# Weighted sums of layer 0: transposes by VectorE in squares of 32 instead of by TensorE, and steps in other units

## The chip, the cores and the metric

The kernel runs on one core of a Trainium2 chip, in float32 throughout. The metric is the time of one execution on the device in microseconds (us); the median of several runs counts. The core's engines work side by side, each through its own queue in program order, and wait for one another through semaphores: TensorE (PE in the profile; its weight loads are PEld), VectorE (DVE), ScalarE (ACT), GpSimd (POOL) and SyncE (SP), which here only issues DMAs. TensorE's results land in PSUM[...]; the other data are in SBUF.

## The reference

The model has two layers, each an attention and a feed-forward part with a layernorm ahead and a residual sum behind. The change lies in the first attention:

```
def _L0_attn_ref(x, Wqkv, bqkv, Wout, bout):      # 16 heads of 8
    B, S, D = x.shape                             # 16, 256, 128
    qkv = (x @ Wqkv + bqkv).reshape(B, S, 3, NUM_HEADS, HEAD_DIM)
    qkv = jnp.transpose(qkv, (2, 0, 3, 1, 4))
    q, k, v = (qkv[0] * SCALE, qkv[1], qkv[2])
    scores = jnp.einsum('bhqd,bhkd->bhqk', q, k)
    attn = jax.nn.softmax(scores, axis=-1)
    out = jnp.einsum('bhqk,bhkd->bhqd', attn, v)
    out = jnp.transpose(out, (0, 2, 1, 3)).reshape(B, S, D)
    return out @ Wout + bout
...
    x = L0_attn_x
    x = x + _L0_attn_ref(_layernorm(x, axis=-1), L0_attn_Wqkv, ...)
    x = x + _L0_ffn_ref(_layernorm(x, axis=-1), ...)
```

The feed-forward part of layer 0 is a gated recurrence over the batch index: from one batch of 256 rows to the next, `c = sigmoid(f) * c + sigmoid(i) * tanh(g)`, where f, i and g are products of the normalised rows and of the old `c` with weights. Each batch thus needs three gates, and the `c` of the batch before. The second layer (linear attention with rotary positions, then a mixture of experts) is not touched.

## The kernel before

The first stage takes the attention of layer 0 and the recurrence together, as a pipeline over 16 batches. An outer loop over `n` runs from -3 to 17, and an inner one over eight units (the table `UNITS`, lines 470 to 479). In each unit `scores` (L333) is issued first, and then the steps that the table lists for that unit; an entry such as `(project, -1)` is `project` for batch n-1. The program is issued in just this order (`manual_schedule`), so the table fixes each engine's order.

`scores` does a quarter of a group of heads at a time, twice. For batch n+1 it computes queries by keys (`pm`, L352, eight matmul records on TensorE in 32-row strips) and VectorE takes each query's maximum from it (`nmax`, L363). For batch n it computes keys by queries with the maxima in an extra row (`psc`, L358), and ScalarE takes the exponential (`pr`, L369). `pm` and `psc` share the pool `ps_me`: three buffers of two PSUM banks each, two of which are taken in each unit.

The other two banks are the pool `ps_x`, two buffers with the tag `misc`, through which everything else goes in turn:

- `stats` (L288): loads x three batches ahead (SP), takes mean and variance (VectorE L213, L214), the root (GpSimd L215, L216), and `xb` = x plus output bias (GpSimd L295). `normal` (L299) normalises (L222, VectorE), `flip` (L302) transposes (L233, TensorE; L234, ScalarE).
- `queries_keys` (L306): two matmuls (L310, L311), two ScalarE copies `qc` and `kc`, nine DMAs from SP which lay them out for `scores`. `values` (L323): two matmuls (L327) and a copy.
- `place_maxima` (L371): two transposes into `pt` (L376), a ScalarE copy `nmT` (L381), two DMAs from SP.
- `weighted` (L387): for four heads at a time, 16 matmul records `av` (L393). Heads lie 32 partitions apart; of each 32 rows, eight are weighted sums, the ninth is the sum of the weights (a column of ones in `va`), and the others are zero. ScalarE copies `av` into `oT` (L400).
- `divide` (L402): for each half of the 256 rows four transposes by TensorE into `po` (L408), then VectorE takes the reciprocal of the ninth columns (L413) and multiplies (L414) into `at`. `flip_heads` (L419) transposes `at` back on TensorE, and ScalarE copies it into `aT`.
- `project` (L423): two matmuls with `wo1` (L427), plus `xb` (VectorE L430) into `xr`, and the statistics of the next layernorm with the same helper as `stats`. `normal2` and `flip2` are as `normal` and `flip`.
- `gate` (L443): two matmuls (L445, L446; two records each) and a tanh on ScalarE. `forget` (L452, VectorE L454) and `update` (L458, VectorE L461 and L464) carry `c` on.

Then follows one product with the final `c` and the second layer, whose order a planner sets by costs.

Of the kernel before, what the change touches and what calls it, by code (L numbers as in the profile page):

```python
# [9 lines left out]
F32 = mybir.dt.float32  # L10
AF = mybir.ActivationFunctionType
ALU = mybir.AluOpType
# [3 lines left out]
B, S, D = 16, 256, 128  # L16
HEADS, HD = 16, 8
NG, GH, ROW = 4, 4, 32
GAP = ROW // HD
P = 128  # L20
NC_ = S // P
E, H, NHC = 16, 256, 2
# [88 lines left out]
def kernel(ctx: ExitStack, tc: tile.TileContext, a: dict, out: bass.AP):  # L111
    nc = tc.nc
# [28 lines left out]
    bv = load("bv", [P, 1])  # L141
    wo1 = load("wo1", [P, D])
    bo1 = load("bo1", [P, D], a["bo1"].partition_broadcast(P))
# [39 lines left out]
    ident = const.tile([P, P], F32, tag="ident", name="ident")  # L183
# [23 lines left out]
    def ln_stats(small, src):  # L207
        st = small.tile([P, NC_, 6], F32, tag="ln_st", name="ln_st")
        mv = small.tile([P, NC_, 2], F32, tag="ln_mv", name="ln_mv")
        ve = small.tile([P, NC_], F32, tag="ln_ve", name="ln_ve")  # L210
        rs = small.tile([P, NC_], F32, tag="ln_rs", name="ln_rs")
        for c in range(NC_):
            nc.vector.bn_stats(st[:, c, :], src[:, c, :])  # L213
            nc.vector.bn_aggr(mv[:, c, :], st[:, c, :])  # L214
        nc.gpsimd.tensor_scalar_add(ve, mv[:, :, 1], EPS)  # L215
        nc.gpsimd.tensor_tensor(rs, ve, mhalf, ALU.pow)  # L216
        return mv, rs

    def ln_apply(work, src, mv, rs, tag):
        y = work.tile([P, NC_, D], F32, tag=tag, name=tag)  # L220
        for c in range(NC_):
            nc.vector.tensor_scalar(  # L222
                y[:, c, :], src[:, c, :], mv[:, c, 0:1], rs[:, c : c + 1], ALU.subtract, ALU.mult
            )
        return y

    def layernorm(small, work, src, tag):
        return ln_apply(work, src, *ln_stats(small, src), tag)

    def transposed(ps_pool, src, dst):  # L230
        ps = ps_pool.tile([P, 512], F32, tag="misc", name="ps_tr")
        for c in range(NC_):
            nc.tensor.transpose(ps[:, c * P : (c + 1) * P], src[:, c, :], ident)  # L233
        nc.scalar.copy(dst, ps[:, :S])  # L234
# [7 lines left out]
    with ExitStack() as st:  # L242
        heads = st.enter_context(tc.tile_pool(name="heads", bufs=1))
        small = st.enter_context(tc.tile_pool(name="small", bufs=3))
        work = st.enter_context(tc.tile_pool(name="work", bufs=2))
# [3 lines left out]
        ps_x = st.enter_context(tc.tile_pool(name="ps_x", bufs=2, space=PSUM))  # L249
# [36 lines left out]
        now = {}  # L286
# [10 lines left out]
            )  # L297

        def normal(b):  # L299
            now["y1", b] = ln_apply(work, *now.pop(("ln1", b)), "ln1")  # L300

        def flip(b):  # L302
            yT = now["yT", b] = work.tile([P, S], F32, tag="yT", name="yT")
# [83 lines left out]
        def weighted(b, g):  # L387

            prs = [now.pop(("pr", b, 2 * g + i)) for i in range(2)]
            av = ps_x.tile([P, S], F32, tag="misc", name="av")  # L390
            for c in range(NC_):
                for j in range(GH):
                    nc.tensor.matmul(  # L393
                        av[ROW * j : ROW * (j + 1), :], lhsT=vas[b % 3][:, c, GH * g + j, :],
                        rhs=prs[j // 2][:, j % 2, c, :],
                        start=(c == 0), stop=(c == NC_ - 1),
                    )
            if g == 0:
                now["oT", b] = work.tile([P, NG, S], F32, tag="oT", name="oT")
            nc.scalar.copy(now["oT", b][:, g], av)  # L400

        def divide(b):  # L402
            oT = now.pop(("oT", b))
            at = now["at", b] = work.tile([P, NC_, D], F32, tag="at", name="at")
            for c in range(NC_):
                po = ps_x.tile([P, HEADS, ROW], F32, tag="misc", name="po")
                for g in range(NG):
                    nc.tensor.transpose(  # L408
                        po[:, GH * g : GH * (g + 1), :].rearrange("p h r -> p (h r)"),
                        oT[:, g, c * P : (c + 1) * P], ident,  # L410
                    )
                rden = small.tile([P, HEADS], F32, tag="rden", name="rden")
                nc.vector.reciprocal(rden, po[:, :, HD])  # L413
                nc.vector.tensor_tensor(  # L414
                    at[:, c].rearrange("p (h d) -> p h d", d=HD), po[:, :, 0:HD],
                    rden.unsqueeze(2).to_broadcast([P, HEADS, HD]), ALU.mult,
                )

        def flip_heads(b):  # L419
            aT = now["aT", b] = work.tile([P, S], F32, tag="aT", name="aT")  # L420
            transposed(ps_x, now.pop(("at", b)), aT)

        def project(b):  # L423
            aT = now.pop(("aT", b))
# [6 lines left out]
            now["ln2", b] = xr[:, b], *ln_stats(small, xr[:, b])  # L431

        def normal2(b):
            now["y2", b] = ln_apply(work, *now.pop(("ln2", b)), "ln2")

        def flip2(b):
            transposed(ps_x, now.pop(("y2", b)), xT2[:, b])
# [20 lines left out]
        def update(b):  # L458
# [10 lines left out]

        UNITS = (  # L470
            ((weighted, -1, 3), (flip, 2), (forget, -2)),
            ((place_maxima, 0, 1), (divide, -1)),
            ((weighted, 0, 0), (flip_heads, -1), (stats, 3)),
            ((queries_keys, 2), (values, 2), (normal, 3)),
            ((weighted, 0, 1), (project, -1)),
            ((place_maxima, 1, 0), (gate, -2, 2), (normal2, -1)),
            ((weighted, 0, 2), (flip2, -1), (update, -2)),
            ((gate, -1, 0), (gate, -1, 1)),
        )
        with tc.manual_schedule():  # L480
            for n in range(-3, B + 2):
# [21 lines left out]
    with ExitStack() as st:  # L503
        small = st.enter_context(tc.tile_pool(name="small1", bufs=3))
# [29 lines left out]
        now = {}  # L534
# [599 lines left out]
    with ExitStack() as st:  # L1134
# [4 lines left out]
        now = {}  # L1139
# [72 lines left out]
def _laid_out(inp):  # L1212

    import numpy as np

    f = np.float32

    g = {k: np.asarray(v) for k, v in inp.items()}
    a = {"x": g["L0_attn_x"]}
    w, bias = g["L0_attn_Wqkv"], g["L0_attn_bqkv"]  # L1220
    a["wq"], a["wk"], a["wv"] = w[:, :D], w[:, D : 2 * D], w[:, 2 * D :]
    a["bq"], a["bk"], a["bv"] = (bias[i * D : (i + 1) * D, None] for i in range(3))
    a["wo1"], a["bo1"] = g["L0_attn_Wout"], g["L0_attn_bout"]

    gates = ("f", "i", "c")
    a["wg"] = np.stack([g[f"L0_ffn_w{i}"].T for i in gates], 1)
    a["ug"] = np.stack([g[f"L0_ffn_u{i}"].T for i in gates], 1)
    a["bg"] = np.stack([g[f"L0_ffn_b{i}"] for i in gates], 1)
    a["in_c"] = g["L0_ffn_in_c"][:, None]
    a["woT"], a["uoT"], a["bo"] = g["L0_ffn_wo"].T, g["L0_ffn_uo"].T, g["L0_ffn_bo"]  # L1230

    w = g["L1_attn_w_qkv"].T
    wq = w[:, :D].reshape(D, HEADS, 2, HD // 2)
    a["wq2"] = np.stack([wq.reshape(D, D), wq[:, :, ::-1].reshape(D, D)], 1)
    wk = w[:, D : 2 * D].reshape(D, HEADS, 2, HD // 2)
    a["wk2"] = np.concatenate([wk.reshape(D, D), wk[:, :, ::-1].reshape(D, D)], 1)
    a["wv2"] = w[:, 2 * D :]
    a["wo2"] = g["L1_attn_w_out"].T
    inv = (1.0 / f(10000.0) ** (np.arange(0, HD, 2, dtype=f) / f(HD))).astype(f)
    ang = np.arange(S, dtype=f)[:, None] * inv[None, :]  # L1240
    cos, sin = np.cos(ang).astype(f), np.sin(ang).astype(f)
    cos, sin = np.concatenate([cos, cos], 1), np.concatenate([-sin, sin], 1)
    turn = np.stack([cos, sin], 1)
    a["turnN"] = turn.reshape(NC_, P, 2, HD).transpose(1, 0, 2, 3)
    a["turnT"] = np.tile(turn.transpose(2, 1, 0) * f(HD**-0.5), (HEADS, 1, 1))
    head = np.arange(D) // HD
    a["bmask"] = np.concatenate(
        [head[:, None] == head[None, :], head[:, None] == np.arange(HEADS)[None, :]], 1
    ).astype(f)

    a["desc"] = np.arange(E, 0, -1).astype(f)
    a["wr"], a["br"] = g["L1_ffn_Wr"], g["L1_ffn_br"]
    a["b2"] = np.zeros((P, GT, D), f)
    for i in range(GT):
        a["b2"][i * E : (i + 1) * E, i] = g["L1_ffn_b2"]
    a["wx"] = np.concatenate(
        [
            g["L1_ffn_b1"].reshape(E, NHC, P).transpose(2, 0, 1),
            g["L1_ffn_W1"].transpose(1, 0, 2),
            g["L1_ffn_W2"].reshape(E, NHC, P, D).transpose(2, 0, 1, 3).reshape(P, E, NHC * D),  # L1260
        ],
        2,
    )
    n = np.arange(P, dtype=f)
    a["before"] = (n[:, None] < n[None, :]).astype(f)
    a["upto"] = (n[:E, None] <= n[None, :E]).astype(f)
    a["steps128"] = P * n[: 2 * E, None]
    a["numbers"], a["numbers128"] = n[:, None], P * n[:, None]
    a["first_row"], a["which"] = REGION * n[:E], n[:E]
    a["seen0"] = REGION // P * n[:E]  # L1270
    a["gap_row"] = (P // 8 * (n % 8))[:, None]
    a["eighth"] = (n[:, None] // 8 == n[None, :E]).astype(f)
    return {k: np.ascontiguousarray(v) for k, v in a.items()}
# [18 lines left out]
```

## Time and profile before

| What | Value |
|---|---|
| Median of three runs | 728.3 us (727.92 to 728.5) |
| The profiled execution | 768.04 us |
| Its span, first to last instruction | 766.3 us |
| Mean granted TensorE clock in it | 0.922 |
| TensorE busy | 616.0 us |
| VectorE busy | 430.4 us |
| ScalarE busy | 384.8 us |
| GpSimd busy | 230.2 us |

The profile is of one execution. It gives the busy time of each engine, the span in 40 slices with the busy share of each in tenths, a chain of waits followed back from the end, and groups of instructions: line, engine, operation, what is written and read, shape, count, then the sum and the mean time of one, and last the idle time ahead of it with what ended it. The timeline gives single instructions: start and duration in us, engine, line, operation, and in square brackets the idle time ahead. The profiled execution is 5% longer than the runs' median, so what is counted in it is set against its own 768.0 us.

### The profile page before, as it was taken

What the parts mean: (1) busy time and instruction counts of PE and PEld (TensorE: products, weight loads), DVE (VectorE), ACT (ScalarE), POOL (GpSimd) and SP (SyncE); (2) the same over time, 40 slices, a digit from 0 to 9 for tenths busy, and PEclk for the clock granted to TensorE, in tenths of its full rate; (3) what the DMA queues carried; (4) which work ended last, traced back from release to release, by engine and by line L of the source; (5) the groups of instructions that cost most, each with busy time, mean ns of one, the idle gap of its engine ahead of it and who ended that gap; (6) DMA issues with size and microseconds to landing.
All of it is one profiled execution on the core that took longest, in us unless ns stands there. A gap on an engine that the chain in (4) does not pass through costs nothing.

```text
span 766.3 us, 15741 instructions
## 1 busy us (share of the span) xinstructions
PE 616.0 (80%) x5452; PEld 456.5 (60%) x5452; DVE 430.4 (56%) x1147; ACT 384.8 (50%) x944; POOL 230.2 (30%) x326
## 2 busy tenths in 40 slices
PE   2699999999999999999959999789666676677620
PEld 1455566666666666665548888678533566676620
DVE  6546676667766676666245786877443333332314
ACT  1045656666666665665525665545211466565620
POOL 6000110111111010100012337367374355556530
PEclk9779999999999999999999999999765699998975
DMA  5100222200000000000000001011012222232238
GB/s 136 52 22 21 74 76 78 71 25 24 23 24 21 12 12 17 16 17 2 2 0 1 1 1 36 11 40 35 25 43 80 71 75 77 75 81 70 71 90 241
DMA packets 45734, 35.42 MB, mean 46 GB/s; under 512 B 9575, under 2 KB 42604, under 8 KB 45016
## 3 DMA queue, kind: packets, MB, share of 16 engines
q1 hardware_dynamic: 39752, 24.57, 12.1%
q0 software_dynamic: 4752, 9.54, 3.8%
q8 instruction: 43, 0.70, 0.4%
q10 hardware_dynamic: 1152, 0.33, 0.2%
q14 instruction: 35, 0.29, 0.1%
HBM read 18.01 MB, written 12.66 MB: 40 GB/s over the span
## 4 chain that ended last, share of the span: by engine, by line
PE 75%; DVE 6%; issue 5%; ACT 5%; DMA 5%; SPq 2%; another core or an unknown queue 1%; POOL 0%; ACTq 0%; DVEq 0%; POOLq 0%
PE pm L352 15%; PE av L393 8%; PE ph L1164 5%; PE py L1175 5%; PE psc L358 5%; PE pt L1155 3%; PE pg L445 3%; PE pg L446 3%; PE ps_tr L233 2%; PE bank_v L650 2%; DMA z<-zd 2%; PE pk L614 2%; PE pq L608 1%; PE po L408 1%; PE po L427 1%
## 5 line engine op out<-in xcount | busy, mean ns | idle before, releaser
L363 DVE TENSOR_REDUCE nmax<-pm 128x4 f32<-128x1024 f32 x128 | 156.1, 1222 | 100.8 <-PE psc L358 92.6
L369 ACT ACTIVATE pr<-psc 128x1024 f32<-128x1024 f32 x128 | 131.0, 1024 | 135.8 <-PE psc L358 135.8
L352 PE MATMUL pm<-ka,qa 32*128 32x256 f32 x1024 | 160.8, 415 | 5.5 <-DMA ka<-kc 4.9
L358 PE MATMUL psc<-qa,ka 32*128 32x256 f32 x1024 | 147.9, 407 | 3.6 <-DVE nmax L363 2.7
L352 PEld LDWEIGHTS pm<-ka,qa 32*128 32x128 f32 x1024 | 101.5, 192 | 33.8 <-issue 26.8
L215 POOL TENSOR_SCALAR ln_ve<-ln_mv 128x2 f32<-128x2 f32 x32 | 7.0, 219 | 335.8 <-DVE ln_mv L214 335.8
L358 PEld LDWEIGHTS psc<-qa,ka 32*128 32x128 f32 x1024 | 91.0, 188 | 10.7 <-DVE nmax L363 6.5
L1185 POOL DMA_INDIRECT zd<-zs,to x80 | 78.0, 975 | 64.5 <-ACT xT L1157 44.8
L1149 DVE COPY w<-wx 128x514 f32 x80 | 35.9, 448 | 92.6 <-PE pt L1155 55.2
L1164 PE MATMUL ph<-xT,w 128*128 128x128 f32 x320 | 53.7, 292 | 31.7 <-ACT xT L1157 31.5
L946 POOL DMA_INDIRECT xd<-rows,sloti x64 | 64.1, 1001 | 24.8 <-issue 15.7
L393 PE MATMUL av<-pr,va 128*32 128x256 f32 x1024 | 69.4, 389 | 1.1 <-ACT pr L369 1.1
L1164 PEld LDWEIGHTS ph<-xT,w 128*128 128x128 f32 x320 | 44.5, 201 | 37.1 <-ACT xT L1157 37.1
L1175 PE MATMUL py<-w,h 128*128 128x128 f32 x320 | 53.5, 291 | 6.8 <-issue 3.6
L1169 ACT ACTIVATE h<-ph,w 128x128 f32<-128x128 f32 x160 | 51.4, 381 | 14.3 <-PE ph L1164 5.2
L1175 PEld LDWEIGHTS py<-w,h 128*128 128x128 f32 x320 | 44.5, 198 | 9.2 <-ACT h L1169 4.3
L1180 ACT ACTIVATE zs<-py,xs 128x128 f32<-128x128 f32 x80 | 30.8, 386 | 37.3 <-PE pt L1155 32.2
L393 PEld LDWEIGHTS av<-pr,va 128*32 128x32 f32 x1024 | 26.9, 110 | 34.0 <-issue 16.7
L445 PE MATMUL pg<-xT,wg 128*128 128x256 f32 x96 | 30.4, 398 | 0.5 <-ACT xT L234 0.5
L446 PE MATMUL pg<-c,uh 128*128 128x256 f32 x96 | 28.5, 379 | 0.0
L1157 ACT COPY xT<-pt 128x128 f32<-128x128 f32 x80 | 22.9, 286 | 11.0 <-PE pt L1155 11.0
L408 PE MATMUL po<-ident,oT 128*128 128x128 f32 x128 | 20.1, 280 | 9.8 <-ACT nmT L381 9.7
(199 smaller groups left out, 1133.8 us busy)
## 6 DMA issues: line engine op xcount, KB each, us to landing
xs<-xd SPq DMA_DIRECT2D x80, 65.0 KB
wx<-in_wx_dram SPq DMA_DIRECT2D x4, 1028.0 KB
z<-zd SPq DMA_DIRECT2D x16, 256.0 KB
x<-in_x_dram SPq DMA_DIRECT2D x16, 128.0 KB
qa<-qc SPq DMA_DIRECT2D x64, 32.0 KB
ka<-kc SPq DMA_DIRECT2D x64, 32.0 KB
out_dram<-fin SPq DMA_DIRECT2D x8, 256.0 KB
zd<-zs,to POOLq DMA_INDIRECT x80
```

Of the source, the lines that this page charges most:

```text
L352: nc.tensor.matmul(pm[:, n, c], lhsT=qm[r, gm, cols], rhs=km[r, gm, :], start=True, stop=True,)
L358: nc.tensor.matmul(psc[:, n, c], lhsT=ke[r, ge, cols], rhs=qe[r, ge, :], start=True, stop=True,)
L363: nc.vector.tensor_reduce(now["nmax", bm][:, :, gm, jm : jm + 2].rearrange("p c j -> p j c"), pm, AX.X, ALU.max, negate=True,)
L369: nc.scalar.activation(pr, psc, AF.Exp)
L393: nc.tensor.matmul(av[ROW * j : ROW * (j + 1), :], lhsT=vas[b % 3][:, c, GH * g + j, :], rhs=prs[j // 2][:, j % 2, c, :], start=(c == 0), ...
L445: nc.tensor.matmul(pg, lhsT=wg[:, i], rhs=xT2[:, b], start=True, stop=False)
L446: nc.tensor.matmul(pg, lhsT=uh[:, i], rhs=now["c2", b - 1], start=False, stop=True)
L946: put = nc.gpsimd.indirect_dma_start(xd, bass.IndirectOffsetOnAxis(ap=t["sloti"][:, c, i : i + 1], axis=0), now["rows", q][:, c, i, :], No ...
L1164: nc.tensor.matmul(ph[:, c], lhsT=w[:, W1_AT + c * P : W1_AT + (c + 1) * P], rhs=xT, start=True, stop=True,)
L1169: nc.scalar.activation(h[:, c], ph[:, c], AF.Gelu, bias=w[:, c : c + 1])
L1175: nc.tensor.matmul(py, lhsT=h[:, c], rhs=w[:, W2_AT + c * D : W2_AT + (c + 1) * D], start=(c == 0), stop=(c == NHC - 1),)
L1185: put = nc.gpsimd.indirect_dma_start(zd, bass.IndirectOffsetOnAxis(ap=to, axis=0), zs, None, bounds_check=2 * SLOTS - 1, oob_is_err=False,)
```

## The change

`weighted` no longer has ScalarE copy `av`. VectorE reads it from PSUM and transposes it in squares of 32 into `ow`, so that partition p of quarter j holds, for each of eight blocks of 32 rows, one row of head 4g+j: eight sums and the sum of weights. `divide` takes all reciprocals at once (32 for each partition), multiplies into `aw`, whose columns are ordered by block, group and place in the head, and transposes in squares of 32 again into `aT`; TensorE does none of it. `flip_heads` is gone. In `aT` the rows are then ordered otherwise (place in the group ahead of group), and the rows of `wo1` and `bv` are put in that order on the host.

`normal` runs on GpSimd instead of VectorE; `normal2` stays on VectorE. In the table, `project` moves from unit 4 to unit 2, where `flip_heads` was; `values` from unit 3 to unit 4; and gate 1 of a batch from unit 7, beside gate 0, to unit 1 of the next turn of `n`.

```
-    def ln_apply(work, src, mv, rs, tag):
+    def ln_apply(work, src, mv, rs, tag, eng):
...
-            nc.vector.tensor_scalar(
+            eng.tensor_scalar(
...
-            now["y1", b] = ln_apply(work, *now.pop(("ln1", b)), "ln1")
+            now["y1", b] = ln_apply(work, *now.pop(("ln1", b)), "ln1", nc.gpsimd)
...
-                now["oT", b] = work.tile([P, NG, S], F32, tag="oT", name="oT")
-            nc.scalar.copy(now["oT", b][:, g], av)
+                now["ow", b] = work.tile([P, NG, SQ, ROW], F32, tag="ow", name="ow")
+
+            nc.vector.transpose(now["ow", b][:, g].rearrange("p i r -> p (i r)"), av)
 
         def divide(b):
-            oT = now.pop(("oT", b))
-            at = now["at", b] = work.tile([P, NC_, D], F32, tag="at", name="at")
-            for c in range(NC_):
-                po = ps_x.tile([P, HEADS, ROW], F32, tag="misc", name="po")
-                for g in range(NG):
-                    nc.tensor.transpose(
-                        po[:, GH * g : GH * (g + 1), :].rearrange("p h r -> p (h r)"),
-                        oT[:, g, c * P : (c + 1) * P], ident,
-                    )
-                rden = small.tile([P, HEADS], F32, tag="rden", name="rden")
-                nc.vector.reciprocal(rden, po[:, :, HD])
-                nc.vector.tensor_tensor(
-                    at[:, c].rearrange("p (h d) -> p h d", d=HD), po[:, :, 0:HD],
-                    rden.unsqueeze(2).to_broadcast([P, HEADS, HD]), ALU.mult,
-                )
-
-        def flip_heads(b):
+
+            ow = now.pop(("ow", b))
+            rden = small.tile([P, NG, SQ], F32, tag="rden", name="rden")
+            nc.vector.reciprocal(rden, ow[:, :, :, HD])
+            aw = work.tile([P, SQ, NG, HD], F32, tag="aw", name="aw")
+            nc.vector.tensor_tensor(
+                aw.rearrange("p i g d -> p g i d"), ow[:, :, :, 0:HD],
+                rden.unsqueeze(3).to_broadcast([P, NG, SQ, HD]), ALU.mult,
+            )
             aT = now["aT", b] = work.tile([P, S], F32, tag="aT", name="aT")
-            transposed(ps_x, now.pop(("at", b)), aT)
+            nc.vector.transpose(aT, aw.rearrange("p i g d -> p (i g d)"))
...
-            now["y2", b] = ln_apply(work, *now.pop(("ln2", b)), "ln2")
+            now["y2", b] = ln_apply(work, *now.pop(("ln2", b)), "ln2", nc.vector)
...
             ((weighted, -1, 3), (flip, 2), (forget, -2)),
-            ((place_maxima, 0, 1), (divide, -1)),
-            ((weighted, 0, 0), (flip_heads, -1), (stats, 3)),
-            ((queries_keys, 2), (values, 2), (normal, 3)),
-            ((weighted, 0, 1), (project, -1)),
+            ((place_maxima, 0, 1), (gate, -2, 1), (divide, -1)),
+            ((weighted, 0, 0), (project, -1), (stats, 3)),
+            ((queries_keys, 2), (normal, 3)),
+            ((weighted, 0, 1), (values, 2)),
             ((place_maxima, 1, 0), (gate, -2, 2), (normal2, -1)),
             ((weighted, 0, 2), (flip2, -1), (update, -2)),
-            ((gate, -1, 0), (gate, -1, 1)),
+            ((gate, -1, 0),),
...
-    a["wo1"], a["bo1"] = g["L0_attn_Wout"], g["L0_attn_bout"]
+
+    a["bv"], a["wo1"] = (
+        v.reshape(NG, GH, HD, -1).transpose(1, 0, 2, 3).reshape(D, -1)
+        for v in (a["bv"], g["L0_attn_Wout"])
+    )
+    a["bo1"] = g["L0_attn_bout"]
```

## What I predict, and from what

> **What bounds the kernel now.** I read the page first: the slices and the chain of waits for where layer 0 lies and who holds it, the groups for the price of each operation. Then the waits of 45 to 345 us, and the timeline of one batch at 193 to 219 us for the order within it.
>
> ```profile
> PE   2699999999999999999959999789666676677620
> DVE  6546676667766676666245786877443333332314
> PEclk9779999999999999999999999999765699998975
> ...
> PE 75%; DVE 6%; issue 5%; ACT 5%; DMA 5%; SPq 2%; another core or an unknown queue 1%; POOL 0%; ACTq 0%; DVEq 0%; POOLq 0%
> ...
> L363 DVE TENSOR_REDUCE nmax<-pm 128x4 f32<-128x1024 f32 x128 | 156.1, 1222 | 100.8 <-PE psc L358 92.6
> ```
>
> A slice is 19.2 us. Layer 0's attention fills slices 2 to 19 (to about 394 us): TensorE at 9 throughout, its clock full, VectorE at 6 to 7. So TensorE looks like the bound, and VectorE's reduce waits for it.
>
> The timeline shows that this is half the truth:
>
> ```profile
> 202.06 1.23 DVE L363 TENSOR_REDUCE nmax<-pm 128x4 f32<-128x1024 f32 x1 [0.85 <-PE psc L358]
> 203.69 0.42 DVE L430 TENSOR_TENSOR xr<-po,xb 128x256 f32<-128x256 f32 x1 [0.40 <-PE po L427]
> 204.14 0.29 DVE L213 BATCH_NORM_STATS2 ln_st<-xr 128x6 f32<-128x128 f32 x1
> ...
> 204.87 0.18 DVE L214 BATCH_NORM_AGGREGATE ln_mv<-ln_st 128x2 f32<-128x6 f32 x1
> 204.97 1.19 DVE L363 TENSOR_REDUCE nmax<-pm 128x4 f32<-128x1024 f32 x1
> ```
> ```profile
> 195.22 0.66 PE L408 MATMUL po<-ident,oT 128*128 128x128 f32 x4 [0.65 <-ACT nmT L381]
> ...
> 205.83 0.69 PE L352 MATMUL pm<-ka,qa 32*128 32x256 f32 x2
> 206.22 0.48 PE L358 MATMUL psc<-qa,ka 32*128 32x256 f32 x1
> ```
>
> In each unit the score matmuls fill two of the three double-bank buffers `pm`/`psc`, so the next unit's `psc` needs the buffer that this unit's `nmax` frees. At 205.83 `pm` goes, and `psc` stands until 206.22, just after `nmax` ended at 204.97+1.19 = 206.16. From a unit's first `psc` to the next one's there are thus two paths:
> - VectorE: `nmax` starts 1.18 later (204.97 was later still, behind the statistics), takes 1.22, and 0.06 after it `psc` goes: **2.46 us at least**.
> - TensorE: about 1.07 of scores and what the unit adds. The timeline's starts give 1.0 for `av`, 0.37 for a pair of transposes with its drain, 0.97 for queries and keys, 0.54 for values, 0.64 for the projection, 0.97 for a gate, 0.21 for `pt`.
>
> The first `psc` of units 2, 3, ... lies at 195.81, 198.29, 200.87, 203.59, 206.22, 208.67, 211.67, 214.13, 217.28. Steps of units 0 to 7: 2.47, 3.13, 2.47, 2.58, 2.72, 2.63, 2.46, 3.00; sum **21.46 us a batch**, the same in every batch. Only units 1, 3, 4 and 7 are TensorE's; eight VectorE paths would be 19.7.
>
> [...] No transpose by VectorE is in this trace; nearest rows are from PSUM: `xr` 425 ns for 256 columns, `nmax` 1222 for 1024, 1.04 ns an element[...]. [...] the two L222 at 11.92 us took 2.58 beside GpSimd's 1.82 us memset of 12.53, and 0.60 at 206.18 without it.
>
> **The change part by part**, times from a unit's first `psc`, profile's durations.
>
> *TensorE* loses 8 `po` transposes, their wait of 0.65 for `nmT`, and 2 of `at`. Unit 1: `pt`, gate 1: 1.07+0.21+0.97 = 2.25 (was 3.13). Unit 2: `av`, projection: 2.72, as unit 4 now. Unit 3: queries and keys: 2.04. Unit 4: `av`, values: 2.62. Unit 7: one gate: 2.04 (was 3.00). Units 0, 5, 6 as before.
>
> *ScalarE* loses five copies of 0.37 a batch. It waited 113.1 us for `psc`; worth nothing.
>
> *VectorE* loses 2x(0.25+0.29) and the two L222 of 0.60 for `x`; it gets five transposes, a reciprocal of 32 columns (row L413: 0.25 for 16) and a product of 256 with both inputs in SBUF (row L461: 0.42). Transpose of 256 columns: [...] I take **0.43**, the `xr` row. An operation that needs nothing from the one before starts 0.08 before that one ends (`nmax` at 197.00 takes 1.23, the next operation starts at 198.15), so `nmax` holds VectorE for 1.15 and a transpose for 0.35; where it needs the result, 0.03 to 0.05 comes on top.
>
> Unit by unit, VectorE's next `nmax` is wanted at step+1.18:
> - 0: `nmax` 1.18, transpose 2.33 (`av` is there at 2.21, as ScalarE's copy shows), `keep_c` 2.68, free 3.04; wanted 3.65.
> - 1: 2.33, reciprocal 0.28, product 0.45, transpose 0.35: free 3.41; wanted 3.64. `aT` is ready 1 us before the projection needs it.
> - 2: transpose 2.33 to 2.68; `xr` waits for `po` until 2.82 (203.69 minus 200.87); +0.45; statistics of `xr` 0.83 (204.14 to 204.97); those of `x`, which stay here, 0.81 (198.15 to 198.96): free **4.91**, wanted 2.72+1.18 = 3.90. The next `nmax` is 1.0 late.
> - 3: so `nmax` starts at 2.19, takes 1.19, +0.06: step **3.44** instead of 2.46. This is where the pile of unit 2 is paid.
> - 4: free 2.68, no wait. 5: L222 twice, free 2.92.
> - 6: transpose, `add_c` 0.45, `c` 0.36: free 3.49, wanted 3.64. 7: nothing.
>
> Steps 2.47, 2.46, 2.72, 3.44, 2.62, 2.46, 2.47, 2.46: **21.10**, 0.36 less a batch. What TensorE is spared (about 2 us) mostly turns into waits for `nmax`.
>
> Batches with n = 1 to 12: 12x0.36 = 4.3. With n = 13 and 14 there is no `x` to take statistics of: `nmax` of unit 3 starts at 1.38, step 2.63, batch 20.29: 1.2 and 1.05 less. n = 15 has no `pm`: unit 1 loses 0.8, unit 2 gains 0.27, unit 4 loses 0.64 (a softmax wait of ScalarE eats part), unit 7 loses 0.97: about 2.0. After it the chain from the last `av` (ends 381.9) to the projection (384.66), now copy, 8 transposes, reciprocal, product, 2 transposes, copy, becomes transpose, reciprocal, product, transpose: 0.9 less. Together 2.9. Sum 4.3+2.2+2.9 = **9.4 us**.
>
> *GpSimd* gets L222 for `x`: row L215 (219 ns for 2 columns) plus 126 columns[...]. `flip` wants it five units later; with 2.55 us busy in 20 its queue has room, and even 1 us each would be hidden. [...] The projection's `ve` and `rs` now go ahead of those of `x` (0.93 later, same slack).
>
> *Buffers and queues.* `av` in `ps_x` (two buffers) is freed at 2.76 by VectorE; the next user in unit 3 writes at 3.8. Steps that issue DMAs (`stats`, `queries_keys`, `place_maxima`) stay in their units, so SP's order stays. Start: SP issues q at 20.83 though `qc` is ready at 18.23; an earlier y1 brings nothing. The reordered rows of `wo1` and `bv` cost nothing.
>
> The profiled execution took 768.0 us; minus 9.4 is 758.6. The runs' median is 728.3; the page doesn't show where those 40 us lie (its slices of low clock lie before 58 and after 530 us, not in the repeating batches). I take the same 9.4 off: **719**.
>
> **Rivals.**
> - A, a transpose costs about 0.8 (twice the rate): in unit 2 0.23 more before `xr`, unit 7 late by 0.2, unit 1 near: batch 21.65, 12x0.19 - 1.1 - 2.2 = -1.0, i.e. 727. [...]
> - B, slower: the pile in unit 2 is longer than the gain, because the transpose from PSUM takes 1.0 to 1.2. Then every place above shifts: batch 22.25 to 23.0, 736 to 747. It decides from 0.83 on. [...] for it that no row shows the operation and that unit 2's queue has no slack left.
> - C, the pile hides (statistics overlap more): every step at its floor, 20.1: 14x1.36+2.9 = 22 less, 706. Against it: VectorE's order is fixed, and 204.97 shows `nmax` waiting behind just such statistics.
>
> **How the numbers follow.** Forecast 0.66 (own range 714 to 724: 0.2 us a batch either way, 1 us at the end), A 0.12, B 0.18, C 0.04. Under 0.2% (1.5 us) this kernel can't be told from no change: A splits into 0.03, 0.05, 0.04. Faster 0.73, same 0.05, slower 0.22. The range 713 to 735 takes in the forecast, A and the lower edge of B.
>
> **What would show it.** Right: transposes at 0.4 to 0.5, step of unit 3 near 3.4 and no `po<-ident` left, other units at 2.46 to 2.7; `psc` waiting for `nmax` in most units. Wrong: transposes above 0.6, a batch above 21.5, units 1 or 7 over 2.6, `xr` later than 2.82, or L222 on GpSimd delaying `flip`.

## The result and the profile after

The changed kernel takes 720.77 us (median of 17 runs, 717.38 to 726.93) against 727.41 us for the kernel before, taken in the same set of runs: a ratio of 0.991, 95% interval 0.9887 to 0.9933, so 6.6 us less (4.9 to 8.2). The forecast was 719, from 728.3.

The profiled execution of the changed kernel took 717.38 us, that of the kernel before 768.04. Most of that difference isn't the change's. From the end of layer 0's last product with `c` to the end of the program, three profiles of the kernel before took 371.2, 363.2 and 328.4 us, three of the changed one 325.0, 324.3 and 324.4. In three further sets of runs the kernel before had medians of 772.77, 765.74 and 727.70 us, while the steps of its batches n = 1 to 12 agreed to 0.01 us in its three profiles (executions of 768.04, 760.49 and 728.36 us). So runs are compared here only as ratios within a set, and layer 0 by its own times. Why the second layer varies was not sought.

The page of the changed kernel, in the parts shown of before: slices (17.9 us each), shares of the chain, groups.

```profile
PE   2799999999999999999996998999885669888800
DVE  4346677777777777777744577889774445444414
PEclk9999999999999999999999999999995569999955
...
PE 63%; DVE 12%; DMA 9%; issue 5%; POOL 5%; ACT 3%; DVEq 2%; SPq 1%; POOLq 0%; ACTq 0%
PE pm L350 12%; PE av L391 9%; PE psc L356 9%; DMA zd<-zs,to 5%; PE pg L436 3%; DVE nmax L361 3%; PE pg L437 3%; DMA z<-zd 2%; PE ph L1155 2%; PE py L1166 2%; POOL xd L937 2%; PE ps_tr L231 2%; DVE ln_st L214 2%; PE po L418 1%; PE pk L605 1%
...
L361 DVE TENSOR_REDUCE nmax<-pm 128x4 f32<-128x1024 f32 x128 | 156.2, 1222 | 94.4 <-PE psc L356 79.6
...
L356 PE MATMUL psc<-qa,ka 32*128 32x256 f32 x1024 | 147.6, 407 | 12.0 <-DVE nmax L361 12.0
...
L399 DVE STREAM_TRANSPOSE ow<-av 128x256 f32<-128x256 f32 x64 | 28.2, 441 | 12.5 <-PE av L391 12.5
```

The chain covers the second layer too, so its sums by engine say little here; but it now runs through `nmax` (3%) and the statistics (2%), neither of which is among the lines of the chain before. TensorE still shows 9 in nearly every slice, but `psc` now stands 12.0 us for `nmax`. The waits from 45 to 345 us, 14 batches, say the same (total us, times, longest), with the weight load of `psc` (PEld) beside it, first before, then changed:

```profile
DVE nmax L363 <- PE psc L358: 84.4, 99, 2.2
...
PEld psc L358 <- DVE nmax L363: 3.0, 3, 1.3
PE psc L358 <- DVE nmax L363: 1.8, 3, 0.9
```
```profile
DVE nmax L361 <- PE psc L356: 75.7, 74, 2.2
...
PEld psc L356 <- DVE nmax L361: 17.4, 18, 1.4
...
PE psc L356 <- DVE nmax L361: 10.4, 16, 1.0
```

Each engine waits for the other, at different places in the batch. The list counts only idle time, 16 to 18 waits of `psc` in these 14 batches; a `psc` that stands while records of `pm` fill TensorE isn't in it. The starts show more: in the mean of n = 1 to 12, the next unit's `psc` begins 0.05 us after a unit's `nmax` ends in six of the changed kernel's eight units (0.31 after units 2 and 4). Before, this was so in four (0.05 to 0.06; in the others 0.18 to 0.73). Where `psc` waits longest is seen on VectorE's timeline of units 2 and 3 of one batch:

```profile
198.34 1.23 DVE L361 TENSOR_REDUCE nmax<-pm 128x4 f32<-128x1024 f32 x1
199.48 0.44 DVE L399 STREAM_TRANSPOSE ow<-av 128x256 f32<-128x256 f32 x1
199.97 0.42 DVE L421 TENSOR_TENSOR xr<-po,xb 128x256 f32<-128x256 f32 x1
...
201.16 0.18 DVE L215 BATCH_NORM_AGGREGATE ln_mv<-ln_st 128x2 f32<-128x6 f32 x1
201.25 0.26 DVE L214 BATCH_NORM_STATS2 ln_st<-x 128x6 f32<-128x128 f32 x1
201.62 0.18 DVE L215 BATCH_NORM_AGGREGATE ln_mv<-ln_st 128x2 f32<-128x6 f32 x1
...
202.11 1.19 DVE L361 TENSOR_REDUCE nmax<-pm 128x4 f32<-128x1024 f32 x1
204.54 1.23 DVE L361 TENSOR_REDUCE nmax<-pm 128x4 f32<-128x1024 f32 x1 [1.23 <-PE psc L356]
```

and on TensorE's of the same time:

```profile
199.87 0.48 PE L356 MATMUL psc<-qa,ka 32*128 32x256 f32 x1
...
202.00 0.69 PE L350 MATMUL pm<-ka,qa 32*128 32x256 f32 x2
203.36 0.48 PE L356 MATMUL psc<-qa,ka 32*128 32x256 f32 x1 [0.66 <-DVE nmax L361]
```

Unit 3's `psc` starts at 199.87, and its maxima are wanted 1.18 later, at 201.05. VectorE is still on the statistics of unit 2 until 202.11, without a gap. `nmax` then ends at 203.30, `psc` of unit 4 follows at 203.36, and VectorE has nothing to do for 1.23 us. Unit 3 takes 3.48 us in place of 2.58.

Steps of a batch (first `psc` of a unit to that of the next, mean of n = 1 to 12), in us:

| | 0 | 1 | 2 | 3 | 4 | 5 | 6 | 7 | batch |
|---|---|---|---|---|---|---|---|---|---|
| before | 2.47 | 3.13 | 2.47 | 2.58 | 2.72 | 2.63 | 2.46 | 3.00 | 21.46 |
| forecast | 2.47 | 2.46 | 2.72 | 3.44 | 2.62 | 2.46 | 2.47 | 2.46 | 21.10 |
| after | 2.46 | 2.46 | 2.72 | 3.48 | 2.72 | 2.47 | 2.46 | 2.46 | 21.27 |

The last row gives unit 3 as it is in most batches. Its batch is 0.04 above the sum, since unit 3 took 3.81 in n = 5 and 3.56 in n = 1, in each of the three profiles. (In n = 5 of the first, VectorE stands 0.21 us between two statistics of x; the profile names nothing that it waits for.) Layer 0 as a whole, in the first profile of each, to the end of the product with the final `c`:

| Part | Forecast, us less | Measured, us less |
|---|---|---|
| start, to the first `psc` of n = 0 | 0 | -3.1 (37.91 to 41.02) |
| n = 0 | in "start" | 0.1 |
| n = 1 to 12 | 4.3 | 2.35 |
| n = 13 and 14 | 2.2 | 2.64 (1.08 and 1.56) |
| n = 15 and what follows to that product | 2.9 | 2.58 |
| sum | 9.4 | 4.6 (395.07 to 390.49) |

Over three profiles of each kernel the product ends at 396.1 and 390.9 on average, 5.3 less. What the runs show beyond that, 1.3 us, is less than the half width of their interval (1.7) and was not traced; the stretch behind the product, named above, differs by more than that in the profiles of one set (328.4 before, 324.3 and 324.4 changed).

### The profile page after: what moved, and what is told of

The parts are those of the page before. It is cut to its first block, busy times and chain, and to the rows that moved or that the text cites. A ratio compares the mean times of both kernels' runs of the same rounds, so it can differ in the third digit from the quotient of the medians.

```text
span 715.5 us, 15431 instructions
## 1 busy us (share of the span) xinstructions
PE 600.9 (84%) x5292; PEld 437.8 (61%) x5292; DVE 446.9 (62%) x1163; ACT 362.5 (51%) x864; POOL 257.3 (36%) x358
## 4 chain that ended last, share of the span: by engine, by line
PE 63%; DVE 12%; DMA 9%; issue 5%; POOL 5%; ACT 3%; DVEq 2%; SPq 1%; POOLq 0%; ACTq 0%
PE pm L350 12%; PE av L391 9%; PE psc L356 9%; DMA zd<-zs,to 5%; PE pg L436 3%; DVE nmax L361 3%; PE pg L437 3%; DMA z<-zd 2%; PE ph L1155 2%; PE py L1166 2%; POOL xd L937 2%; PE ps_tr L231 2%; DVE ln_st L214 2%; PE po L418 1%; PE pk L605 1%
## 5 line engine op out<-in xcount | busy, mean ns | idle before, releaser
L350 PE MATMUL pm<-ka,qa 32*128 32x256 f32 x1024 | 177.3, 425 | 5.3 <-DMA ka<-kc 5.3
L350 PEld LDWEIGHTS pm<-ka,qa 32*128 32x128 f32 x1024 | 111.1, 196 | 38.2 <-issue 28.5
L1176 POOL DMA_INDIRECT zd<-zs,to x80 | 79.5, 993 | 33.9 <-ACT xT L1148 12.0
L1140 DVE COPY w<-wx 128x514 f32 x80 | 39.8, 497 | 47.2 <-PE pt L1146 22.0
L1155 PEld LDWEIGHTS ph<-xT,w 128*128 128x128 f32 x320 | 43.0, 195 | 14.0 <-ACT xT L1148 13.6
L1166 PE MATMUL py<-w,h 128*128 128x128 f32 x320 | 49.5, 277 | 0.2
L1166 PEld LDWEIGHTS py<-w,h 128*128 128x128 f32 x320 | 42.6, 194 | 0.7 <-ACT h L1160 0.7
L399 DVE STREAM_TRANSPOSE ow<-av 128x256 f32<-128x256 f32 x64 | 28.2, 441 | 12.5 <-PE av L391 12.5
```

The lines of the kernel that those rows point to most:

```text
L350: nc.tensor.matmul(pm[:, n, c], lhsT=qm[r, gm, cols], rhs=km[r, gm, :], start=True, stop=True,)
L1155: nc.tensor.matmul(ph[:, c], lhsT=w[:, W1_AT + c * P : W1_AT + (c + 1) * P], rhs=xT, start=True, stop=True,)
L1166: nc.tensor.matmul(py, lhsT=h[:, c], rhs=w[:, W2_AT + c * D : W2_AT + (c + 1) * D], start=(c == 0), stop=(c == NHC - 1),)
L1176: put = nc.gpsimd.indirect_dma_start(zd, bass.IndirectOffsetOnAxis(ap=to, axis=0), zs, None, bounds_check=2 * SLOTS - 1, oob_is_err=False,)
```

## The experiments

Three theories stood against each other. T1: each unit takes the longer of TensorE's own work and the path through `nmax`, which includes what VectorE still has in its queue. T2: the sum of TensorE's work counts, and 2 us of transposes and waits saved simply gave less than hoped. T3: VectorE's total work became the bound. Diffs are against the changed kernel.

**The change in two halves.** First the transposes alone, with every step in its old unit (and `normal` on GpSimd); then with gate 1 moved too. The second differs from the changed kernel only in `project` and `values`.

```
-            ((place_maxima, 0, 1), (gate, -2, 1), (divide, -1)),
-            ((weighted, 0, 0), (project, -1), (stats, 3)),
-            ((queries_keys, 2), (normal, 3)),
-            ((weighted, 0, 1), (values, 2)),
+            ((place_maxima, 0, 1), (divide, -1)),
+            ((weighted, 0, 0), (stats, 3)),
+            ((queries_keys, 2), (values, 2), (normal, 3)),
+            ((weighted, 0, 1), (project, -1)),
...
-            ((gate, -1, 0),),
+            ((gate, -1, 0), (gate, -1, 1)),
```

> VectorE's transposes and GpSimd's normal as in the changed kernel, but project in unit 4, values in unit 3 and gate 1 in unit 7, as before the change. Theory 1 (from a unit's first psc to the next one's the longer of TensorE's work and of the path by nmax, with whatever VectorE has queued ahead of nmax, counts): nothing piles up in unit 2 any more, steps 2.46, 2.46, 2.46, 2.58, 2.72, 2.63, 2.46, 3.00, a batch of 20.8 us against 21.25 of the changed kernel; some 3.5 us faster than the changed kernel, some 10 us (ratio 0.986) faster than before. Theory 2 (the sum of TensorE's work sets the time): TensorE does the same work as in the changed kernel, so the time is the same as its, ratio 0.991.

> As transposes_alone, and gate 1 of a batch in unit 1 of the next turn. Theory 1: unit 7 falls from 3.00 to 2.46 and unit 1 stays at 2.46, a batch of 20.2 us; some 11 us faster than the changed kernel, 18 us faster than before, ratio about 0.975. Theory 2: same work on TensorE, ratio 0.991.

Measured: 0.9893 (0.9857 to 0.9929), batch 20.80, units 1 and 7 at 2.46 and 3.00; and 0.9729 (0.9682 to 0.9777), batch 20.25, unit 7 at 2.46. So of the 0.2 us that a batch gains, 0.66 comes from the transposes (with `normal` on GpSimd), 0.55 from gate 1, and 1.02 is lost again by `project` and `values`: they cost more than the transposes brought. TensorE does the same work in the changed kernel and in the second of these, yet 0.991 stands against 0.973. The changed kernel was compared in another set, but one with the same TensorE order in this set (below, `normal` back on VectorE) has 0.992. T2 falls. From the waits of the second kernel, same window as above, where 17.4 us stood:

```profile
PEld psc L356 <- DVE nmax L361: 5.6, 6, 1.3
```

**The statistics of x out of the pile.** `project` and `values` stay where the change put them; `stats` moves from unit 2 to 4, `normal` from 3 to 5.

```
-            ((weighted, 0, 0), (project, -1), (stats, 3)),
-            ((queries_keys, 2), (normal, 3)),
-            ((weighted, 0, 1), (values, 2)),
-            ((place_maxima, 1, 0), (gate, -2, 2), (normal2, -1)),
+            ((weighted, 0, 0), (project, -1)),
+            ((queries_keys, 2),),
+            ((weighted, 0, 1), (values, 2), (stats, 3)),
+            ((place_maxima, 1, 0), (gate, -2, 2), (normal2, -1), (normal, 3)),
```

> The changed kernel with the statistics of x moved from unit 2 to unit 4 and normal from unit 3 to unit 5. Theory 1: nmax of unit 3 is late by 0.2 instead of 1.05 us, step of unit 3 2.63 instead of 3.48, unit 4 has room for the 0.81 us; a batch of 20.4 us, some 10 us faster than the changed kernel, ratio to before about 0.976. Theory 2, or if another thing than VectorE's pile holds psc in unit 3: same as the changed kernel, 0.991.

Measured: 0.9781 (0.9748 to 0.9815), batch 20.38, unit 3 at 2.63, all others as in the changed kernel. VectorE's timeline:

```profile
195.13 0.18 DVE L215 BATCH_NORM_AGGREGATE ln_mv<-ln_st 128x2 f32<-128x6 f32 x1
195.23 1.19 DVE L361 TENSOR_REDUCE nmax<-pm 128x4 f32<-128x1024 f32 x1
197.66 1.23 DVE L361 TENSOR_REDUCE nmax<-pm 128x4 f32<-128x1024 f32 x1 [1.24 <-PE psc L356]
```

`nmax` follows the statistics of `xr` at once, 0.86 earlier in its unit than in the changed kernel. The same 0.8 us of VectorE's work, done two units later, costs nothing there. This is what T1 says, and T3 doesn't.

**`normal` back on VectorE**, one argument (`nc.gpsimd` to `nc.vector`).

> The changed kernel with normal back on VectorE. Theory 1: its 0.59 us stand behind nmax in unit 3, where VectorE has 1.2 us to spare; the batch stays at 21.25 us and the time within 1.5 us of the changed kernel, ratio 0.991. Theory 3 (VectorE's total work matters): 0.59 us a batch more, 9 us slower than the changed kernel, ratio 1.003.

Measured: 0.992 (0.9891 to 0.9948), no different from the changed kernel's 0.991; batch 21.17. About 1 us more for VectorE in each batch (twice 0.521; 0.59 had been expected) lengthens none: against T3 again. Unit 3 is even 0.07 shorter, since the first statistics of x take 0.29 from start to start here and 0.37 in the changed kernel (201.25 to 201.62 above). What slows them there was not isolated.

**One transpose twice, in two places.** The transpose of `av` is done a second time, into the same place, for `g == 0` (unit 2), and in the other kernel for `g == 1` (unit 4).

```
             nc.vector.transpose(now["ow", b][:, g].rearrange("p i r -> p (i r)"), av)
+            if g == 0:
+                nc.vector.transpose(now["ow", b][:, g].rearrange("p i r -> p (i r)"), av)
```

> The changed kernel with the transpose of av in unit 2 done twice, so 0.44 us more of VectorE ahead of xr and the statistics. Theory 1: xr starts 0.2 to 0.4 us later (0.13 us of slack before it), and the step of unit 3 becomes longer by just that, 3.7 to 3.9 instead of 3.48; a batch of 21.5 to 21.6 us. If VectorE's added work is hidden, 21.25.

> The changed kernel with the transpose of av in unit 4 done twice: the same 0.44 us more of VectorE, in a unit where it is free 1.2 us before nmax is wanted. Theory 1: no step changes, a batch of 21.25 us. Theory 3 (VectorE's total work matters): 21.6 to 21.7 as with unit 2.

Each is a single execution. In unit 2, unit 3's step grows from 3.48 to 3.80; in unit 4 no step changes. The two timelines:

```profile
201.95 0.45 DVE L401 STREAM_TRANSPOSE ow<-av 128x256 f32<-128x256 f32 x1
202.32 0.38 DVE L423 TENSOR_TENSOR xr<-po,xb 128x256 f32<-128x256 f32 x1
```
```profile
207.18 0.45 DVE L401 STREAM_TRANSPOSE ow<-av 128x256 f32<-128x256 f32 x1
208.29 1.23 DVE L361 TENSOR_REDUCE nmax<-pm 128x4 f32<-128x1024 f32 x1 [0.66 <-PE psc L356]
```

The first pushes `xr` and all that follows; the second ends in a gap that is still 0.66 long. The same instruction has the price of its place. The 0.32 is less than the 0.45 of the transpose: `xr` starts 0.37 after the second transpose does, before its end. It lies 3.17 into the unit in place of 2.82, and takes 0.38 in place of 0.42.

**Spread.** If T1 holds, `project` and `values` in halves should fit under the path through `nmax` in every unit. Halves of `project` go to units 2 and 4, of `values` to 3 and 7, `stats` to 3, `normal` to 5.

```
-        def values(b):
+        def values(b, c):
...
-        def project(b):
+        def project(b, c):
...
-            ((weighted, 0, 0), (project, -1), (stats, 3)),
-            ((queries_keys, 2), (normal, 3)),
-            ((weighted, 0, 1), (values, 2)),
-            ((place_maxima, 1, 0), (gate, -2, 2), (normal2, -1)),
+            ((weighted, 0, 0), (project, -1, 0)),
+            ((queries_keys, 2), (values, 2, 0), (stats, 3)),
+            ((weighted, 0, 1), (project, -1, 1)),
+            ((place_maxima, 1, 0), (gate, -2, 2), (normal2, -1), (normal, 3)),
...
-            ((gate, -1, 0),),
+            ((gate, -1, 0), (values, 2, 1)),
```

> A table made by Theory 1: values and projection split into their two halves of 128 rows, the projection's halves in units 2 and 4, those of values in units 3 and 7, statistics of x in unit 3, normal in unit 5, gate 1 in unit 1. Theory 1: in no unit is TensorE's work longer than 2.46 us, and VectorE is free before the next nmax is wanted everywhere (unit 2: transpose, half of xr and its statistics free at about 3.4, wanted 3.64; unit 3: statistics of x free at 3.14), so all eight steps at 2.46, a batch of 19.7 us; some 18 us faster than the changed kernel, 25 us faster than before, ratio about 0.965. Theory 2 (TensorE's work): two more evictions, the same work on TensorE, ratio 0.991.

Measured: 0.9699 (0.9646 to 0.9751), batch 19.78, steps 2.46, 2.46, 2.50, 2.47, 2.50, 2.47, 2.46, 2.46: within 0.1 us of eight paths through `nmax`. VectorE's timeline shows unit 2's half of the projection done before the maxima are due:

```profile
189.54 0.44 DVE L398 STREAM_TRANSPOSE ow<-av 128x256 f32<-128x256 f32 x1
189.91 0.25 DVE L423 TENSOR_TENSOR xr<-po,xb 128x128 f32<-128x128 f32 x1
...
190.91 1.23 DVE L360 TENSOR_REDUCE nmax<-pm 128x4 f32<-128x1024 f32 x1 [0.20 <-PE psc L355]
```

This beats both kernels. Its matmuls are those of the changed one; only the copy of `values` and the sum `xr` come in halves. Its product with the final `c` ends at 372.74, where the kernel before, in the same set, has 395.48.

**The start.** The table of parts leaves 3 us at the start unexplained, where the forecast had nothing. Four more executions were profiled to see whether it repeats: one of the kernel before in the second of the three further sets, and one of it and two of the changed kernel in the third.

> The kernel before once more, for its profile. If TensorE's clock at the start differs from execution to execution, its first psc of n = 0 can lie anywhere between 37.9 us, as in the first profile, and the 39.7 to 41.8 us of the five changed kernels profiled so far. If the change itself makes the start later, it lies at 37.9 again. Batches of 21.46 us either way.

> The kernel before, a third profile of its start. If the clock's early rise at 29 us belongs to this kernel: first psc of n = 0 at 38 us again. If it is chance: in some execution 40 to 42.

> The changed kernel, a second profile of its start. If the later start belongs to the change: first psc of n = 0 at 41 us again. If it is chance: in some execution 38.

> As after_second, a third profile: 41 us if the later start belongs to the change, 38 in some execution if it is chance.

First `psc` of n = 0 over all profiles, in us:

| `values` | kernels | first `psc` of n = 0 |
|---|---|---|
| whole, in unit 3 | before, three times | 37.91, 38.36, 39.76 |
| whole, in unit 3 | transposes alone; with gate 1 moved | 39.67, 39.87 |
| half in unit 3 | spread | 40.13 |
| in unit 4 | changed, three times | 41.02, 41.20, 41.78 |
| in unit 4 | `stats` in unit 4; `normal` back | 40.88, 41.81 |
| in unit 4 | a transpose twice, unit 2; unit 4 | 41.32, 41.54 |

No value of one kind reaches the other. Up to this moment the changed kernel and the one with gate 1 moved differ in the place of `values` alone, so the later start goes with that place. It doesn't go with the engine of `normal`, which is VectorE at 41.81 and GpSimd at 39.67. TensorE's timelines of two kernels in the third set, first before, then changed:

```profile
32.22 0.86 PE L327 MATMUL pv<-wv,yT 128*128 128x128 f32 x4
33.01 1.16 PE L352 MATMUL pm<-ka,qa 32*128 32x256 f32 x16
34.10 0.38 PE L376 MATMUL pt<-ident,nmax 128*8 128x128 f32 x2
...
39.76 0.76 PE L358 MATMUL psc<-qa,ka 32*128 32x256 f32 x1 [2.45 <-DMA qa<-nmT]
```
```profile
32.69 2.08 PE L350 MATMUL pm<-ka,qa 32*128 32x256 f32 x8
34.70 1.22 PE L325 MATMUL pv<-wv,yT 128*128 128x128 f32 x4
35.85 2.08 PE L350 MATMUL pm<-ka,qa 32*128 32x256 f32 x8
...
41.78 0.79 PE L356 MATMUL psc<-qa,ka 32*128 32x256 f32 x1 [0.48 <-DVE nmax L361]
```

Before, the same matmuls get faster at about 33 us: two transposes `pt` take 0.38. In the changed kernel eight `pm` take 2.08 at 35.85, and it is as slow as at 32.69. From the start of queries and keys (30.36 and 30.69) to `pt`, the same work takes 3.74 us in the one and 7.17 in the other; the kernel before then gives a part back, as its `psc` waits 2.45 us for the DMA of the maxima. The windows of 10 us (length, TensorE's busy time and instructions, the clock that TensorE was granted as a share of full speed, DMA share, GB/s), before and changed:

```profile
30.00:40.00 10.00, 7.55 (x50) 0.84 0.11 27
40.00:50.00 10.00, 10.00 (x66) 0.51 0.07 17
```
```profile
30.00:40.00 10.00, 10.00 (x46) 0.50 0.10 26
40.00:50.00 10.00, 9.52 (x57) 0.50 0.01 3
```

All six profiles with `values` or half of it in unit 3 have a stretch of full clock between 29 and 42 us, 3.4 or 6.8 us long; none of the seven with it in unit 4 shows one between 22 and 51 us. In five of these seven, the first of the changed kernel among them, the records of the clock only begin there, so the digit 9 in that page's first slices proves nothing; but the two `pt` of that time take 0.59 in all seven, and 0.38 in the five with `values` whole in unit 3. The stretches of half and of full clock in these records last 3.4, 6.8, 10.2, 13.7 and 30.7 us, multiples of the shortest. What raises or lowers the clock doesn't show in them. From 30 to 40 us the changed kernel's records have TensorE busy for all 10.00 us at a clock of 0.50, those of the kernel before for 7.55 us at 0.84. What these records call busy does not tell the clock. The moment of the rise varied among the six profiles from 28.98 to 34.77.

In the kernel before, `pv` follows right behind queries and keys; in the changed one eight `pm` stand between. In four of the six profiles the clock rises when `pv` has begun (32.74 to 34.77). In the first two of the kernel before, however, it rises at 28.98 and 29.47, ahead of `pv` (30.41 and 30.86). Up to there TensorE's order is the same in the kernel before and in the changed one, so the place of `values` cannot have raised the clock in these two. The first of them:

```profile
26.12 3.39 PE L352 MATMUL pm<-ka,qa 32*128 32x256 f32 x24
...
29.44 0.70 PE L310 MATMUL pqk<-yT,wq 128*128 128x256 f32 x2
```

In the third profile the same records take 3.79 and 1.22. The first two also have the earliest starts, 37.91 and 38.36. The three other profiles with `values` whole in unit 3 start at 39.67 to 39.87, the seven with it in unit 4 at 41.36 on average: some 1.6 us, where the three profiles of each kernel differ by 2.7. That `pv` behind the eight `pm` leaves the clock down was not shown: it is a reading of these records, which no run isolates, and what raised the clock early in two of them stays open.

A last kernel tried to raise the clock from outside: spread, with 4 and 7 matmuls of 384 columns, whose results nobody reads, at the starts of turns n = -3 and -1.

```
+                    if (n, u) == (-3, 0):
+                        busy(4)
+                    if (n, u) == (-1, 0):
+                        busy(7)
```

> The table of spread, and eleven matmuls of 384 columns whose result nobody reads: four after the first matmul of the program, seven ahead of the first pm, where TensorE stands idle from 8 to 14 and from 18 to 23.5 us. If the start is slow because TensorE's clock comes up only at 50 us (pm and pqk at twice their later times), the clock is up before 23 us, the turns n = -1 and n = 0 run at full speed, the first psc of n = 0 lies at 36 us or earlier and that of n = 1 below 57 (spread: 40.1 and 63.6); 6 to 8 us faster than spread, ratio to before about 0.96. If the start is held by DMAs and VectorE instead, no faster than spread, ratio 0.970.

Measured: 0.9648 (0.9613 to 0.9684), 701.80 us against 727.70. This is the lowest ratio of all, though its interval overlaps that of spread; in layer 0 its product with the final `c` ends at 370.69, 2.05 before that of spread. The first `psc` of n = 0 comes at 38.55, of n = 1 at 61.59, where spread had 40.13 and 63.62: 1.6 to 2.0 us gained, not the 4 to 7 that were expected. The full clock came at 22.0 us, but

```profile
34.73 0.69 PE L357 MATMUL pm<-ka,qa 32*128 32x256 f32 x2
38.55 0.76 PE L363 MATMUL psc<-qa,ka 32*128 32x256 f32 x1 [3.13 <-DMA qa<-nmT]
```

TensorE then waits 3.13 us for the DMA that places the maxima, and from 35.7 to 49.3 the clock is half again. So with matmuls added for nothing but the clock the start came earlier (38.55 against 40.13, one profile of each), and the faster start ran into that transfer.

## Why the prediction was right, and where it was off

The direction and the mechanism of the batch were right: most of the saving on TensorE turned into waits for `nmax`, paid in unit 3. The amount was about half of the forecast in layer 0, 4.6 to 5.3 us of 9.4. The runs' 6.6 us lie nearer to it only by the 1.3 us that were not traced; that part of the agreement is luck as far as the record goes.

- *Prices on VectorE.* Right. A transpose of 256 columns took 0.441 from PSUM and 0.445 from SBUF (0.43 was taken), the product 0.426 (0.42). The reciprocal took 0.343, not 0.28; unit 1 had room for it. With this rivals A (0.8) and B (1.0 to 1.2) fall.
- *The pile in unit 2.* Right: `xr` starts 2.82 into the unit, as forecast, VectorE is free at 4.96 (4.91), `nmax` starts 2.24 into unit 3 (2.19), step 3.48 for 3.44. The 0.04 fits the 0.07 by which the statistics of x take longer. Rival C, that the pile hides, falls with it.
- *Unit 4.* Mis-sized: 2.72 for 2.62. The 0.54 for values was read where `pv` follows queries and keys; behind `av` it takes 0.64, as the projection does there (205.43 to 206.07).
- *The batch.* These two and one batch at 3.81 make it 0.20 less, not 0.36: 1.95 us less gained over twelve batches.
- *n = 13 to 15 and the chain behind.* 5.2 us gained, 5.1 forecast. n = 14 gave more (1.56 for 1.05): no values follow, so unit 4 falls to 2.46, and unit 7 took 2.13 where 2.46 was forecast. n = 15 and the tail a little less.
- *The same 9.4 off the shorter runs.* This held: the steps are alike in the executions of 768.04 and 728.36 us.
- *The start.* Here a step failed, the one that took the start as nothing: "an earlier y1 brings nothing". It looked at the DMA of the first q, not at TensorE's work, whose clock is low at that time (7 tenths in the second and third of the slices that it read). The start took 2.7 us longer on the average of three profiles each (41.3 against 38.7), and 3.0 with n = 0 in the first profiles. For these the sum closes: 9.4 - 1.95 - 3.0 + 0.1 for n = 13 to the end is 4.6. That a start with `values` in unit 4 comes later is shown by every profile; how much of the 2.7 us the change caused is not, since two of the three profiles before had a clock that rose ahead of anything that was moved on TensorE.
- *GpSimd.* Its `normal` took 0.798 each, more than the author's estimate but below the 1 us that the forecast had room for, and was hidden all the same: the table's `flip` comes five units later.
- *ScalarE's relief* and the route of `aT` to the projection: worth nothing and not late, as said: ScalarE waits 123.1 us for `psc` where it waited 113.1, and `aT` is ready at 198.30, 0.92 before the projection begins.

## What to carry to other kernels

Where two engines hand buffers to each other in every unit of a loop, cost a change unit by unit, by the later of the two paths: the same 0.44 us instruction cost 0.32 in one unit and nothing in another, and neither engine's sum of work told which. When a move shortens one engine's work, look what queue it lengthens ahead of the next handover, and split or spread steps until each unit fits; here 0.970 was to be had from the matmuls of a kernel at 0.991. Price the start and the end of a pipeline by themselves, since a forecast from the steady batch says nothing of them: here the start was up to 3 us off, a third of the forecast gain.

## What the runs showed of the hardware

- VectorE transposes 128x256 float32 in squares of 32 in 0.44 us, from PSUM or SBUF, about the time of an addition of that size (0.425).
- GpSimd needs 0.798 us to normalise 128x128, where VectorE needs 0.34 on average in the kernel before, and 0.521 in the one with `normal` back on it; for two columns GpSimd needs 0.226.
- With one group of four matmul records moved behind eight others, the same two transposes by TensorE take 0.59 us in seven of seven profiles, and 0.38 in five of five with the group in its old place. Where the clock's records reach back so far, a full clock between 29 and 42 us is missing in the one case and there in the other.
- TensorE's records can fill a stretch of 10.00 us without a gap while the granted clock stays at 0.50 (30 to 40 us in the second and third profile of the changed kernel).
